# Other buffers for the fp8 rounding, a lower rank for the first scan, and earlier loads for the last FFN, in a kernel of four gated layers

## The chip, the cores and the metric

One core of one Trainium2 chip runs the kernel. The metric is the device time of one execution in microseconds; the figure of a kernel is the median over its runs. Of the kernel before there are three: 3698.0, 3705.31 and 3706.08 us, median 3705.31. A profile is one more execution, and it has a time of its own.

## The reference, cut to what matters

The input `x` has 4 batches of 512 rows by 512 columns; a context of 4 x 512 x 256 goes with it. Eight blocks follow one another, and each is added to `x` with a gate:

```python
x = x + tanh(g_xattn[0]) * mamba(ctx, layernorm(x), ...)      # layer 0: a selective scan
x = x + tanh(g_ffn[0])   * ffn_2to4(layernorm(x), ...)        # the two largest of each four kept
x = x + tanh(g_xattn[1]) * attention_from_ctx(layernorm(x))   # layer 1
x = x + tanh(g_ffn[1])   * ffn_ternary(layernorm(x), ...)
x = x + tanh(g_xattn[2]) * mamba(ctx, layernorm(x), ...)      # layer 2: a scan again
x = x + tanh(g_ffn[2])   * ffn_fp8(layernorm(x), ...)         # weights rounded to fp8 e4m3
x = x + tanh(g_xattn[3]) * attention_16_heads(layernorm(x), ctx, ...)   # layer 3
x = x + tanh(g_ffn[3])   * bitlinear_ffn(layernorm(x), ...)   # quantized rows, b1, gelu, layernorm, b2
```

The part of the two `mamba` blocks that is a recurrence (convolution, `u`, `dt`, and 16 states for each of 512 channels over 512 positions) depends on the context alone, not on `x`. So the kernel can compute it at any time before its layer. In the fp8 FFN each weight is rounded to three bits of mantissa (`w.astype(float8_e4m3fn)`). The last FFN works row by row: layer norm, quantization, a product, `b1` and gelu, a layer norm with `gamma` and `beta`, quantization, a second product, `b2`.

## The kernel before, in words

**The main flow** goes over eight stages, called heads: (layer group, batch) in the order (0,0), (0,1), (1,0), (0,2), (1,1), (0,3), (1,2), (1,3). A stage of group 0, `f01`, does the FFN of layer 0, the attention and the FFN of layer 1. A stage of group 1, `f23`, does the fp8 FFN of layer 2 and the attention of layer 3. In the profile the stages begin at about 200, 718, 1137, 1568, 1972, 2399, 2734 and 3158 us; a prologue with the scan of (0,0) stands ahead of them, and a tail from 3584 us, with the last FFN of batch 3, behind them. I call them stage 0 to stage 7.

**Three side lists** run along with the main flow, and `tick(w)`, which the main flow calls after each piece of its own work, feeds them: `side` (the scans of the seven other heads, `mamba_scan`, then the preparation of the last FFN's weights; in stages 6 and 7 the last FFN itself, `l3f`), `pres` (the preparations of the scans, `mamba_pre`) and `prep` (36 fp8 roundings, `to_fp8`, called by `l2f_prep`). Each list has a rate; `tick` adds `w` times the rate to the list's credit and takes steps of the list's generator until the credit is used up. A step costs what its `yield` says. `pres` runs at 0.25, but at 1.0 while the scan that heads `side` still lacks its preparation (`waits()`); `side` at 0.75 takes no step meanwhile but gathers credit; `prep` runs at 0.15. Before a head begins, `finish` traces whatever its scan or preparation still lacks, at once. `nxt.start` (L662 to L666) calls it inside the last product of the FFN of layer 1, then adds the scan's result to `x` (`xmamba`, L649); `nxt.turn` transposes the next input.

**The order in the engines' queues** is not the order of the code. Tile, the compiler layer, schedules all traced instructions with a model of their times: when an engine is free in the model it takes, of the instructions that are ready, the one with the lowest priority number, and that number counts up with each traced instruction. `tick` adds `BEHIND = 1000` to it for `prep`, and for `side` in all stages but the first; `copy` (L247) adds 200 in the first stage and 60 later. On the chip each queue then runs in the order so fixed, and each wait is a semaphore. All loads and most stores are issued by SP, a queue that does nothing else.

**Buffers.** A tile belongs to a tag of a pool, and a tag has a fixed number of buffers. Tag `wr` of pool `wr` (4 buffers of 128x512 f32) takes every raw weight that `unit` loads on its first use (L265), until it is split into a rounded part (ACT, L256) and a rest (POOL and DVE in turn, L257). `to_fp8` takes two of the same four: `raw` (L288) and `m` (L290); it works with DVE (L290), ACT (L293), DVE twice (L294, L295), and stores `raw` with `copy`. Tag `mt` of pool `m` (4 buffers of the same size) belongs to `mamba_pre`: the convolution (L484, L486), `u` (L491), stored to DRAM and loaded again for four matmuls into the bank `xd` (L508), and so on to `dt`, `du` and `y` (L564, L566). The state steps of a scan are L581 (ACT), L582 (POOL), L583 and L584 (DVE), L602 (POOL).

**The last FFN.** `l3f` works on 128 rows, a token tile, at a time. Of a tile's steps the first half goes up to gelu, the second half from there to the store; the first half of one tile is traced in turn with the second half of the tile before. `x` is loaded into `xl` (2 buffers, L1135) just ahead of its use at L359; `b1`, `gamma`, `beta` and `b2` are loaded by `rep` (5 buffers, L1115) just ahead of theirs (L1158, L1188, L1189, L1213). Its weights, 8 tiles, and its token tiles are in one pool, `l3f`. The tail calls the same function with a pool of its own, `tail`, which is opened when the pools of stage 7 are closed.

A pool that is placed on bytes of closed pools waits, as Tile is used here, for every user of those pools.

Of the kernel before, what the change touches and what calls it, by code (L numbers as in the profile page):

```python
# [10 lines left out]
F32 = mybir.dt.float32  # L11
# [12 lines left out]
NT = S // 128  # L24
# [30 lines left out]
BEHIND = 1000  # L55
# [17 lines left out]
def tile_flamingo(ctx: ExitStack, tc: tile.TileContext, I, out):  # L73
# [63 lines left out]
    phase = [0]  # L137

    def tick(w):

        waits = lambda: side and any(k == (*side[0][0], "pre") for k, _ in pres)
        for q, r, i in ((pres, 1.0 if waits() else RATE_PRE, 0), (prep, RATE_FP8, 2), (side, rate[0], 1)):
            credit[i] += w * r
            behind = BEHIND if q is prep or q is side and phase[0] else 0
            while q and credit[i] > 0 and not (q is side and waits()):
                tc.cur_priority += behind
                try:
                    credit[i] -= next(q[0][1])
                except StopIteration:
                    q.pop(0)  # L150
                tc.cur_priority -= behind
            if not q:
                credit[i] = 0.0
# [130 lines left out]
    def to_fp8(dst, src):  # L284


        raw = T(wrp, [128, 512], F32, "wr")
        sy.dma_start(raw, src)  # L288
        m = T(wrp, [128, 512], F32, "wr")
        v.tensor_scalar(  # L290
            m.bitcast(I32), raw.bitcast(I32), 0x7F800000, 0x00400000, op0=ALU.bitwise_and, op1=ALU.bitwise_or
        )
        s.activation(raw, raw, AF.Copy, scale=2.0**-20)  # L293
        v.scalar_tensor_tensor(raw, m, 1.5 * 2.0**-6, raw, op0=ALU.max, op1=ADD)  # L294
        v.scalar_tensor_tensor(raw, m, 1.5 * 2.0**-6, raw, op0=ALU.max, op1=SUB)  # L295
        copy(dst, raw)
# [175 lines left out]
    def mamba_pre(l, b, mp, pp=None):  # L472

        M = lambda tag, shape=(128, 512), dt=F32: T(mp, list(shape), dt, tag)
        po = l * PAR_MW
        ud = []
        for d in range(4):
            if pp:
                xi = xin[l, b, d]
            else:  # L480
                xi = M("mt")
                copy(xi, xin[l, b, d])
            cv = pp.tile([128, 512], F32, tag="cv", name=nm("cv"), bufs=2) if pp else mbps()
            s.activation(cv, xi, AF.Identity, scale=cw[l][:, d * 4 + 3 : d * 4 + 4], bias=cw[l][:, 16 + d : 17 + d])  # L484
            for j in (1, 2, 3):
                v.scalar_tensor_tensor(  # L486
                    cv[:, j:], xi[:, : 512 - j], cw[l][:, d * 4 + 3 - j : d * 4 + 4 - j], cv[:, j:], op0=MUL, op1=ADD
                )
            u = pp.tile([128, 512], F32, name=f"u{d}") if pp else M("mt")
            s.activation(u, cv, AF.Tanh)  # L490
            v.scalar_tensor_tensor(u, u, 1.0, cv, op0=ADD, op1=MUL)  # L491
            if pp:
                ud.append(u)
            else:
                ud.append(dram("u", [128, 512], F32))
                copy(ud[d], u)
            yield 2.6
        xw = M("mt")
        sy.dma_start(xw[:, :320], I[f"M{l}_xp"][0])
        xd = mbps("xd")  # L500
        for d in range(4):
            if pp:
                u = ud[d]
            else:
                u = M("mt")
                copy(u, ud[d])
            c = slice(d * 80, d * 80 + 80)
            pe.matmul(xd[:80], xw[:, c], u, start=d == 0, stop=d == 3)  # L508

        xf = M("mt")  # L510
        s.copy(xf[:80], xd[:80])
        st = M("mt", (128, 512), FR)
        s.copy(st[:80], xd[:80])
        v.tensor_tensor(st[64:80], xd[64:80], st[64:80], op=SUB)
        bcd = dram("bc", [32, 512], F32)
        keep(bcd[0:16], xf[16:32])
        keep(bcd[16:32], xf[48:64])
        dw = unit_dtw(l, mp)
        dtb = lambda d: par[:, po + PAR_M["db"] + d : po + PAR_M["db"] + d + 1]
        Dc = lambda d: par[:, po + PAR_M["D"] + d : po + PAR_M["D"] + d + 1]  # L520
        if pp:
            sc = []
            for d in range(4):
                ps = bank("y", "dtp")
                pe.matmul(ps, dw[:80, 0, d * 128 : d * 128 + 128], st[:80], start=True, stop=True)
                t = pp.tile([128, 512], F32, tag="t", name=nm("t"), bufs=2)
                s.activation(t, ps, AF.Abs, bias=dtb(d))
                s.activation(t, t, AF.Exp, scale=-1.0)
                dt = M("dt")
                s.activation(dt, ps, AF.Relu, bias=dtb(d))  # L530
                ac = pp.tile([128, 512], F32, tag="ac", name=nm("ac"), bufs=2)
                log1p(t, ac, mbps)
                v.scalar_tensor_tensor(dt, ac, LP_K, dt, op0=MUL, op1=ADD)
                du, y = M("du"), M("y")
                g.tensor_tensor(du, dt, ud[d], op=MUL)
                g.tensor_scalar(y, ud[d], Dc(d), 0.0, op0=MUL, op1=ADD)
                sc.append((dt, du, y))
            mst[l, b] = bcd, sc
            return
        ysc[l, b] = [dram("y", [128, 512], F32) for d in range(4)]  # L540
        sc = []
        tmp = dram("dtp", [128, 4, 512], F32)
        for d in range(4):
            ps = mbps("dtp")
            pe.matmul(ps, dw[:80, 0, d * 128 : d * 128 + 128], st[:80], start=True, stop=True)
            x = M("mt")
            s.activation(x, ps, AF.Identity, bias=dtb(d))
            keep(tmp[:, d], x)
        yield 1.0
        for d in range(4):  # L550
            dt = M("mt")
            copy(dt, tmp[:, d])
            t = M("mt")
            s.activation(t, dt, AF.Abs)
            s.activation(t, t, AF.Exp, scale=-1.0)
            s.activation(dt, dt, AF.Relu)
            ac = M("mt")
            log1p(t, ac, mbps)
            v.scalar_tensor_tensor(dt, ac, LP_K, dt, op0=MUL, op1=ADD)
            r = [dram("st", [128, 512], F32) for i in range(2)]  # L560
            copy(r[0], dt)
            u = M("mt")
            copy(u, ud[d])
            g.tensor_tensor(dt, dt, u, op=MUL)  # L564
            copy(r[1], dt)
            g.tensor_scalar(u, u, Dc(d), 0.0, op0=MUL, op1=ADD)  # L566
            copy(ysc[l, b][d], u)
            sc.append(r)
            yield 3.4
        mst[l, b] = bcd, sc  # L570
# [523 lines left out]

    def l3f(b, lp, ws, ps_of=mbps, tail=None):

        nbuf = {"rep": 5, "Y": 2, "q16": 2, "qT": 1, "yT": 4, "sq": 1, "xl": 2}
        if tail:
            nbuf = {"rep": 1, "Y": 4, "q16": 4, "qT": 2, "yT": 8, "sq": 1}

# [3 lines left out]
        def smallL(n):  # L1104
            return lp.tile([128, n], F32, tag="sm", name=nm("sml"), bufs=32 if tail else 16)

        kept = {}

        def rep(n, f):

            if (n, f) in kept:
                return kept[n, f]
            tag = f"rep{n}{f}" if tail else "rep"
            r = lp.tile([128, 512], F32, tag=tag, name=nm("rep"), bufs=nbuf["rep"])
            sy.dma_start(r, I["L3_" + n][512 * f : 512 * f + 512].partition_broadcast(128))  # L1115
            if tail:
                kept[n, f] = r
            return r

        def turned(x, tag):  # L1120

# [7 lines left out]
        def token(t):  # L1129

            if tail:
                x = tail[t]
            else:
                x = L("xl", [128, 512], F32)
                sy.dma_start(x, xsc[b * NT + t])  # L1135
            rs, _ = ln_stats([x], smallL)
            yield 0.7, 1.6
            y = L("Y", [128, 2048], F32)
            z = y[:, 0:512]
            s.activation(z, x, AF.Identity, scale=rs[:, 0:1], bias=rs[:, 1:2])  # L1140
# [11 lines left out]
            for f in range(4):  # L1152
                c = slice(f * 512, f * 512 + 512)
                b1r = rep("b1", f)
                ps = ps_of("l1")
                for k in range(4):
                    pe.matmul(ps, xq[:, k * 128 : k * 128 + 128], ws["w1", k][:, f], start=k == 0, stop=k == 3)  # L1157
                v.scalar_tensor_tensor(y[:, c], ps, sc[:, 1:2], b1r, op0=MUL, op1=ADD)  # L1158
                if f % 2:
                    h = slice((f - 1) * 512, f * 512 + 512)  # L1160
                    s.activation(y[:, h], y[:, h], AF.Gelu, accum_out=m2[:, f // 2 : f // 2 + 1])
                yield 0.7, 1.1
            yield HALF, 0.0

            v.tensor_tensor(m2[:, 2:3], m2[:, 0:1], m2[:, 1:2], op=ADD)
# [14 lines left out]
            for f in range(4):  # L1180
                c = slice(f * 512, f * 512 + 512)
                ga, be = rep("gamma", f), rep("beta", f)
                if tail and f % 2:
                    v.scalar_tensor_tensor(y[:, c], y[:, c], m2[:, 2:3], ga, op0=ADD, op1=MUL)  # L1184
                    v.scalar_tensor_tensor(y[:, c], y[:, c], m2[:, 3:4], be, op0=MUL, op1=ADD)  # L1185
# [32 lines left out]
        gens = [token(t) for t in range(NT)]  # L1218
        if not tail:

            old = iter(())
            for q in gens + [iter(())]:
                new = iter(lambda: next(q, (HALF, 0.0))[0], HALF)
# [76 lines left out]
    mctx.close()  # L1300
    with tc.tile_pool(name="l3f", bufs=2) as lp:
        ws3 = l3f_weights(lp)
        for b in range(2):
            side.append(((b,), l3f(b, lp, ws3)))
        rate[0] = RATES[6]
        f23(heads[6], heads[7])
        finish((1,))
        side.append(((2,), l3f(2, lp, ws3)))
        rate[0] = RATES[7]
        f23(heads[7], None)  # L1310
        finish((2,))
        with psum(t=6), tc.tile_pool(name="tail", bufs=2) as tp2:
            list(l3f(3, tp2, ws3, lambda n: bank("t", n), heads[7].xs))

# [86 lines left out]
```

## Time and profile before

| what | us |
|---|---|
| median of 3 runs | 3705.31 (3698.0 to 3706.08) |
| time of the profiled execution | 3685.68 |
| its span, first to last instruction | 3683.9 |
| busy in the span: PE, DVE, ACT, POOL | 3112.8, 2541.4, 1983.4, 1722.2 |
| mean granted clock of TensorE | 0.928 |

PE is TensorE's matmuls, PEld its weight loads, DVE VectorE, ACT ScalarE, POOL GpSimd, SP the queue that issues DMAs. A line of a group or of the timeline gives line, engine, operation, out<-in. In square brackets of the timeline stands how long the engine was idle before the instruction, and after the arrow what ended that. A line of the table by stage gives, for a stretch of the span, each engine's busy us and its number of instructions, then the granted clock, the share of the DMA engines' time and GB/s.

### The profile page before, as it was taken

How to read it: one execution, taken by the hardware profiler on the slowest of the kernel's cores; microseconds unless marked ns; L12 is line 12 of the kernel's file. 1: busy time of each engine (PE TensorE's matmuls, PEld its weight loads, DVE VectorE, ACT ScalarE, POOL GpSimd, SP SyncE). 2: the span in 40 equal slices, each digit the busy share in tenths (PEclk: the TensorE clock that was granted, in tenths of full speed). 3: DMA queues.
4: the chain of work that ended last, by engine and by line, in shares of the span. 5: the costliest groups of instructions: out<-in, count | busy, mean ns of one | idle time of the engine just before them, and what ended most of it. 6: DMA issues, size and time to landing. Idle time of an engine off the chain costs nothing. (4 is left out here: it accounts for less than half of the span.)

```text
span 3683.9 us, 40258 instructions
## 1 busy us (share of the span) xinstructions
PE 3112.8 (84%) x12216; PEld 1979.4 (54%) x12216; DVE 2541.4 (69%) x4162; ACT 1983.4 (54%) x4405; POOL 1722.2 (47%) x1351
## 2 busy tenths in 40 slices
PE   7785875889778788899888778899999998898985
PEld 3364444565556545475565545475767554564542
DVE  7957856789688787887678878855334455454437
ACT  6455355354545667544544656543435666366644
POOL 5515856637556785744665778700101122222112
PEclk9997887999899899999999899999999999999997
DMA  8577567876876564385676543287664343554310
GB/s 272 186 264 255 182 197 257 287 250 210 272 246 208 189 187 135 108 292 189 211 243 216 169 157 106 90 296 261 227 209 163 120 135 95 166 172 122 110 42 31
DMA packets 310232, 693.10 MB, mean 188 GB/s; under 512 B 31712, under 2 KB 33120, under 8 KB 310016
## 3 DMA queue, kind: packets, MB, share of 16 engines
q1 hardware_dynamic: 256176, 589.86, 47.3%
q10 hardware_dynamic: 53840, 100.68, 9.2%
q8 instruction: 97, 1.59, 0.2%
q14 instruction: 119, 0.97, 0.1%
HBM read 525.46 MB, written 164.95 MB: 187 GB/s over the span
## 5 line engine op out<-in xcount | busy, mean ns | idle before, releaser
L581 ACT ACTIVATE mb<-dt,nA 128x512 f32<-128x512 f32 x512 | 347.1, 689 | 398.2 <-DVE db12x L584 52.0
L333 POOL TENSOR_TENSOR sm<-sm,mhalf 128x8 f32<-128x8 f32 (+4 forms) x96 | 138.8, 1446 | 483.2 <-DVE sm L363 174.1
L678 PE MATMUL gate<-xT,w 128*128 128x512 f32 x624 | 266.9, 428 | 75.4 <-ACT w L256 40.1
L985 PE MATMUL po<-pt,v 128*128 128x512 f32 x512 | 277.9, 631 | 28.3 <-ACT pt L824 22.3
L807 PE MATMUL S<-k,q 128*128 128x512 f32 x512 | 264.9, 620 | 22.2 <-ACT P L814 19.8
L814 ACT ACTIVATE P<-S,st,sm 128x512 f32<-128x512 f32 x256 | 199.9, 783 | 119.1 <-DVE st L812 117.5
L679 PE MATMUL gate<-xT,w 128*128 128x512 f32 x624 | 258.7, 415 | 1.4 <-DVE xT L257 1.4
L402 PE MATMUL acc<-w,hf 128*128 128x512 f32 x512 | 233.0, 614 | 25.6 <-DVE hf L705 14.3
L678 PE MATMUL up<-xT,w 128*128 128x512 f32 x624 | 246.7, 395 | 4.1 <-ACT w L256 4.0
L679 PE MATMUL up<-xT,w 128*128 128x512 f32 x624 | 245.6, 394 | 0.0
L808 DVE TENSOR_REDUCE st<-S 128x1 f32<-128x512 f32 x256 | 173.2, 684 | 92.9 <-PE S L807 91.2
L1003 PE MATMUL down<-wo,h 128*128 128x512 f32 x512 | 231.9, 603 | 0.7 <-DVE x L430 0.7
L333 POOL TENSOR_TENSOR sml<-sml,mhalf 128x1 f32<-128x1 f32 x32 | 18.5, 578 | 440.9 <-DVE sml L1174 229.9
L822 PE MATMUL pT<-ident,P 128*128 128x128 f32 x1024 | 168.7, 285 | 52.0 <-ACT P L814 27.3
L822 PEld LDWEIGHTS pT<-ident,P 128*128 128x128 f32 x1024 | 127.6, 146 | 136.3 <-ACT P L814 45.8
L681 PE MATMUL gate<-xT,w 128*128 128x512 f32 x432 | 181.3, 420 | 14.0 <-POOL w L257 13.8
L678 PEld LDWEIGHTS gate<-xT,w 128*128 128x128 f32 x624 | 125.0, 200 | 116.0 <-ACT w L256 41.8
L402 PEld LDWEIGHTS acc<-w,hf 128*128 128x128 f32 x512 | 99.0, 196 | 155.6 <-issue 113.3
L681 PE MATMUL up<-xT,w 128*128 128x512 f32 x432 | 169.2, 392 | 3.2 <-DVE w L257 3.2
L824 ACT COPY pt<-pT 128x512 f32<-128x512 f32 x256 | 145.9, 589 | 47.7 <-PE pT L822 46.5
L402 PE MATMUL acc<-w,h 128*128 128x512 f32 x352 | 159.7, 606 | 6.3 <-ACT fv L907 4.9
L336 PE MATMUL Q<-w,xT 128*128 128x256 f32 x512 | 156.7, 306 | 3.3 <-ACT xT L256 3.2
(288 smaller groups left out, 8971.9 us busy)
## 6 DMA issues: line engine op xcount, KB each, us to landing
bc<-dbc ACTq DMA_DIRECT2D x105, 512.0 KB, 5.7
w<-dL_g SPq DMA_DIRECT2D x81, 512.0 KB, 5.3
w<-dL_u SPq DMA_DIRECT2D x81, 512.0 KB, 4.6
w<-in_L_d_dram SPq DMA_DIRECT2D x68, 512.0 KB, 5.5
w<-dL_gu SPq DMA_DIRECT2D x48, 512.0 KB, 4.6
w<-dL_q SPq DMA_DIRECT2D x48, 512.0 KB, 5.1
rep<-in_L_b_dram SPq DMA_DIRECT2D x65, 256.0 KB, 3.9
dv<-fv ACTq DMA_DIRECT2D x64, 256.0 KB, 4.0
```

The source lines that it names most:

```text
L333: g.tensor_tensor(a, a, mhalf[:, :n], op=ALU.pow)
L402: pe.matmul(ps, h[:, c], w, start=first, stop=last)
L581: s.activation(ps, dt, AF.Exp, scale=nA[l][:, d * 16 + n : d * 16 + n + 1])
L678: pe.matmul(ps, wh[:, c], xT[k][:, 0], start=k == 0, stop=False)
L679: pe.matmul(ps, wh[:, c], xT[k][:, 1], start=False, stop=wl is None and k == 3)
L681: pe.matmul(ps, wl[:, c], xT[k][:, 0], start=False, stop=k == 3)
L807: pe.matmul(ps, q[:, c], k, start=True, stop=True)
L808: v.tensor_reduce(st[:, t : t + 1], ps, AX.X, ALU.max, negate=True)
L814: s.activation(p, ps, AF.Exp, scale=r, bias=m, accum_out=st[:, 8 + t : 9 + t])
L822: pe.transpose(ps[:, t * 128 : t * 128 + 128], pt[t][:, kt * 128 : kt * 128 + 128], ident)
L985: pe.matmul(po, vs[kt][:, c], u, start=kt == 0, stop=kt == 3)
L1003: pe.matmul(ps, hs[j][:, c], ws[j // 2][:, j % 2], start=j == 0, stop=j == 3)
```

## The change

`tick`: a `side` that waits for its preparation gathers no credit, and the first stage's scan is traced 1000 behind as well.

```diff
         for q, r, i in ((pres, 1.0 if waits() else RATE_PRE, 0), (prep, RATE_FP8, 2), (side, rate[0], 1)):
+            if q is side and waits():
+                continue
             credit[i] += w * r
-            behind = BEHIND if q is prep or q is side and phase[0] else 0
+            behind = BEHIND if q is not pres else 0
```

`to_fp8`: both buffers come from `mt`.

```diff
-        raw = T(wrp, [128, 512], F32, "wr")
+        raw = T(mp, [128, 512], F32, "mt")
         sy.dma_start(raw, src)
-        m = T(wrp, [128, 512], F32, "wr")
+        m = T(mp, [128, 512], F32, "mt")
```

`mamba_pre`: three `u` are loaded a step (2.6) ahead of the matmuls, the fourth a step of 1.3 ahead of its own.

```diff
         xw = M("mt")
         sy.dma_start(xw[:, :320], I[f"M{l}_xp"][0])
+        if not pp:
+
+            for d in range(3):
+                u = M("mt")
+                copy(u, ud[d])
+                ud.append(u)
+            yield 2.6
         xd = mbps("xd")
         for d in range(4):
-            if pp:
-                u = ud[d]
-            else:
+            if not pp and d == 3:
                 u = M("mt")
                 copy(u, ud[d])
+                ud.append(u)
+                yield 1.3
             c = slice(d * 80, d * 80 + 80)
-            pe.matmul(xd[:80], xw[:, c], u, start=d == 0, stop=d == 3)
+            pe.matmul(xd[:80], xw[:, c], ud[d if pp else 4 + d], start=d == 0, stop=d == 3)
```

`l3f`, outside the tail: `xl` has 3 buffers for 2 and `rep` 7 for 5; each vector is loaded one use ahead, `x` of the next token tile ahead of the second half of this one. The token tiles get a pool of their own, `tokens`, on top of the weights' pool, and it is closed before the tail's pool is opened.

```diff
-        nbuf = {"rep": 5, "Y": 2, "q16": 2, "qT": 1, "yT": 4, "sq": 1, "xl": 2}
+        nbuf = {"rep": 7, "Y": 2, "q16": 2, "qT": 1, "yT": 4, "sq": 1, "xl": 3}
...
+        def fetch(*vs):
+
+            if not tail:
+                for n, f in vs:
+                    ahead[n, f] = rep(n, f)
+
+        def fetch_x(t):
+            xls[t] = L("xl", [128, 512], F32)
+            sy.dma_start(xls[t], xsc[b * NT + t])
...
-                x = L("xl", [128, 512], F32)
-                sy.dma_start(x, xsc[b * NT + t])
+                x = xls[t]
             rs, _ = ln_stats([x], smallL)
             yield 0.7, 1.6
+            fetch(("b1", 0))
...
                 b1r = rep("b1", f)
+                if f < 3:
+                    fetch(("b1", f + 1))
...
+            if not tail and t + 1 < NT:
+                fetch_x(t + 1)
+            fetch(("gamma", 0), ("beta", 0))
             yield HALF, 0.0
...
                 ga, be = rep("gamma", f), rep("beta", f)
+                fetch(*((("gamma", f + 1), ("beta", f + 1)) if f < 3 else (("b2", 0),)))
...
+            fetch_x(0)
+            yield 2.0
...
         ws3 = l3f_weights(lp)
-        for b in range(2):
-            side.append(((b,), l3f(b, lp, ws3)))
...
+        with tc.tile_pool(name="tokens", bufs=2) as lq:
+            for b in range(2):
+                side.append(((b,), l3f(b, lq, ws3)))
...
         with psum(t=6), tc.tile_pool(name="tail", bufs=2) as tp2:
             list(l3f(3, tp2, ws3, lambda n: bank("t", n), heads[7].xs))
```

`rep` first looks into `ahead` and takes a vector out of it that has been loaded there.

More of the change, by code (lines that the diff above doesn't have):

```diff
@@ L1105, in smallL @@
             return lp.tile([128, n], F32, tag="sm", name=nm("sml"), bufs=32 if tail else 16)
-        kept = {}
+        kept, ahead, xls = {}, {}, {}
         def rep(n, f):
@@ L1112, in rep @@
                 return kept[n, f]
+            if (n, f) in ahead:
+                return ahead.pop((n, f))
             tag = f"rep{n}{f}" if tail else "rep"
@@ L1302, in tile_flamingo @@
         ws3 = l3f_weights(lp)
-        for b in range(2):
-            side.append(((b,), l3f(b, lp, ws3)))
[L1305 to L1311, printed above, removed]
+        with tc.tile_pool(name="tokens", bufs=2) as lq:
+            for b in range(2):
+                side.append(((b,), l3f(b, lq, ws3)))
+            rate[0] = RATES[6]
+            f23(heads[6], heads[7])
+            finish((1,))
+            side.append(((2,), l3f(2, lq, ws3)))
+            rate[0] = RATES[7]
+            f23(heads[7], None)
+            finish((2,))
         with psum(t=6), tc.tile_pool(name="tail", bufs=2) as tp2:
```

## The prediction

> **What bounds the kernel now.** I read the times of each stage first, then who waited for whom, then the timeline where a wait was long, and last the chain of waits. These are rows of the table by stage: us, then busy us (and instructions) of PE, PEld, DVE, ACT and POOL, the granted clock, the DMA share, GB/s.
>
> ```profile
> 606.00:636.00 30.00, 0.91 (x3) 0.50 (x2) 20.76 (x25) 16.86 (x43) 22.68 (x16) 0.55 0.65 211
> ...
> 718.00:1137.00 419.00, 355.54 (x1276) 236.07 (x1276) 342.97 (x496) 216.38 (x488) 235.40 (x172) 0.93 0.74 247
> ...
> 2399.00:2734.00 335.00, 324.39 (x1252) 224.26 (x1252) 150.22 (x277) 135.76 (x355) 24.12 (x17) 0.99 0.71 243
> 2734.00:3158.00 424.00, 386.92 (x1772) 242.34 (x1772) 209.61 (x495) 251.40 (x563) 90.04 (x78) 0.97 0.45 142
> 3158.00:3584.00 426.00, 396.66 (x1789) 245.21 (x1790) 203.79 (x470) 242.43 (x551) 82.84 (x69) 0.96 0.38 118
> 3584.00:3684.00 100.00, 51.76 (x217) 21.20 (x214) 77.83 (x167) 42.61 (x81) 27.94 (x24) 0.78 0.15 48
> ```
>
> PE bounds the long stages: stage 5 (2399 on), with no scan beside it, is 97% busy. Stages 6 and 7 leave PE idle for 67 of 850 us, and the tail is bound by DVE. Scans lengthen stages 0 to 4. In one stretch, 606 to 636, PE does nothing at all. So a change counts by the PE gaps that it closes or opens; the chain of waits begins only at 3520 us and says nothing of the rest.
>
> **Part 1, fp8 rounding out of the buffers `wr`.** This is the gap of 606, in PE's timeline and then in SP's, DVE's and ACT's:
>
> ```profile
> 605.75 0.40 PE L338 MATMUL K<-fw,fc 128*128 128x512 f32 x1
> 635.24 0.80 PE L678 MATMUL gate<-xT,w 128*128 128x512 f32 x1 [29.09 <-ACT w L256]
> ...
> 604.34 0.43 SPq L288 DMA_DIRECT2D wr<-in_L_u_dram  x1
> ...
> 631.14 0.33 SPq L265 DMA_DIRECT2D wr<-in_L_g_dram  x1
> ...
> 629.48 1.63 DVE L295 SCALAR_TENSOR_TENSOR wr<-wr,wr 128x512 f32<-128x512 f32 x1
> ...
> 634.57 0.62 ACT L256 CAST w<-wr 128x512 fp32r<-128x512 f32 x1 [1.34 <-DMA wr<-in_L_g_dram]
> ```
>
> The gate waits for the split of its weight, the split for the load of 631.14, and that load for the end (631.11) of a rounding whose raw block was asked for at 604.34. Two roundings held all four `wr`. With the roundings in `mt` the gap of 29.1 us goes. What is late next is the scan of (0,1): its last addition on POOL ends at about 630, the last of its products on POOL (L641) starts at 638.2, its result reaches `x` (L649) at 659.5, and the next gates start at 718.4. PE has 66.9 us of work from 606 to 718, so at most 112 - 66.9 = 45 us are to be had.
>
> Against this stands part 2. The scan comes later: its preparation's steps cost 2.6 + 1.3 = 3.9 units more, stage 0 spends some 440 us on 102 units up to `nxt.start` (4.3 us each), hence +17 us; nothing hides that, for `pres` runs at full rate and `side` waits for it. From then the scan needs what it needed: the additions of the seven scans take 207 to 316 us each, at rank 0 (first, 291 us) as at rank +1000 (second, 316 us). I therefore cost the rank at nothing: POOL covers it, which at that rank (stages 1 to 4) is 56 to 73% busy. So the gates of stage 0 end about 627 instead of 657, the product's rows fill PE until 665 (88 matmuls L402, 0.43 us apart: 38 us), `x` gets the scan's result at about 657 (630 + 17, and 10 us for store, load and L641), and the next gates follow 25 to 35 us later, at 682 to 692 (where no scan runs it took 44 us, 2690 to 2734, with PE's rows in between; the 10 to 20 less are my estimate). That is 26 to 36 us less. The roundings now take two of the four `mt` in turn with the preparation; its steps pay some of that back. I take **-25 us**, bounds -45 (PE never idle) and +41 (worked out under the rivals).
>
> The same move in stages 1 and 2 gains nothing, since no raw weight is loaded there, and slows roundings and preparations that share four buffers. The last rounding's L295 runs at 1088, the first gate that needs any at 1137: 49 us of cover. I take **0**, bounds 0 and +25: most roundings run from 826 to 1088, and if sharing stretches these 262 us by 74, the gates wait 74 - 49.
>
> The credit that `side` no longer gathers is 0.75 x 28.9 = 22 of 76.8, about 18 of the 64 state steps; `finish` traces them at `nxt.start`, without the 1000. It is cost at nothing too: POOL's pace sets the scan, not the place in the code. Without that cover they cost 18 x 2.75 us (eight additions in 22 us, the fastest stretch, 338 to 360) = 50 us, behind which PE has 38 us of rows.
>
> **Part 3, `u` ahead.** Before L508 PE and its weight loads sat idle 20.3 us for `mt<-du`, nine times in seven preparations; of the matmuls' own wait 8.6 us is that. A step of 2.6 units is some 10 us, a load lands in about 3 to 4. I take **-5 us**, bounds -15 and +5 (the bank `xd`, one of two for `mb`, is held 1.3 units longer; 11.0 us of waits for it by `db02x` stand in the same row).
>
> **Part 4, the last FFN's loads.** Waits in stages 6 and 7 (us in total, times, longest):
>
> ```profile
> ACT P L814 <- DVE st L812: 70.1, 29, 10.1
> ...
> DVE sml L359 <- DMA xl<-xsc: 47.0, 8, 10.1
> ...
> POOL Y L1188 <- DMA rep<-in_L_gamma_dram: 34.1, 15, 5.6
> ```
>
> One of the eight, in SP's, DVE's and PE's timeline:
>
> ```profile
> 2907.65 0.42 SPq L1215 DMA_DIRECT2D out_dram<-xl  x1
> ...
> 2911.64 0.33 SPq L1135 DMA_DIRECT2D xl<-xsc  x1
> ...
> 2915.54 0.69 DVE L359 BATCH_NORM_STATS2 sml<-xl 128x6 f32<-128x512 f32 x1 [7.91 <-DMA xl<-xsc]
> ...
> 2917.31 1.11 PE L822 MATMUL pT<-ident,P 128*128 128x128 f32 x4 [6.74 <-ACT P L814]
> ```
>
> With two `xl` the load follows the store of the tile before; DVE stands still in its queue, the maximum for the softmax (L808, L812) stands behind it, then ACT's exponential, then PE. A third buffer, loaded half a tile ahead, removes store and load from that. Of PE's gaps over 0.8 us these follow such a wait: 6.74 + 0.85 (2911), 1.27 (3035), 7.61 (3150), 8.89 + 0.85 (3376): 26.2. Behind waits for `b1`: 1.33 + 4.22 (3104, 3113) and 4.09 (3336): 9.6. Together 35.9.
>
> After such a gap the clock is low. In the table by stage the windows 2911:2923, 3150:3162 and 3377:3391 have clocks 0.57, 0.72 and 0.63, and 4.85 + 4.58 + 5.07 = 14.5 us of PE work that would take about half: 7 us more. The Trainium skill, "TensorE: Matmul & The Clock Gate", Part 1, says that for modelling the ramp costs under 1% of a typical span; by that the 7 would be left out and this part's value would be 24. The rows speak against it: the mean clock is 0.928 over the span.
>
> Of 43 us I take two thirds, **-28 us**: DVE's next wait is for PE's scores, and some of PE's gaps would be there a little later. Bounds -43 and 0. SP issues as many transfers as before; with seven `rep` it blocks less.
>
> **Part 5, the tail's pool.** It now lies on `tokens`, so it waits for that pool's last user too. SP's timeline:
>
> ```profile
> 3583.86 1.75 SPq L1115 DMA_DIRECT2D rep<-in_L_b_dram  x4
> ...
> 3588.81 0.34 SPq L1215 DMA_DIRECT2D out_dram<-xl  x1
> ```
>
> Today the tail's loads start as the last product of stage 7 ends (3583.80), its first L359 at 3584.49. The last token tile's store is issued at 3588.81 and lands at 3592.1. Waiting for it costs 3592.1 - 3584.5 = 7.6 us; nothing hides it, as everything in the tail follows. Bounds 0 (the tile done sooner) and +8. I take **+7**.
>
> **Sum:** -25 + 0 - 5 - 28 + 7 = -51 us. The profiled execution took 3685.7 (span 3683.9 and 1.8 around it), so 3635 there. The median lies 19.6 above that execution; I keep this difference: 3705.3 - 51 = **3654 us**.
>
> **Rivals.**
> - *The scan comes too late (slower).* In stage 0 a rounding holds a buffer from its load to the landing of its store, 241.5 to 270.6 = 29 us. If the preparation of (0,1), 247 to 327, has to wait out two of these, its scan starts at 338 + 17 + 58 = 413 and ends, after the same 291 us, at 704, not 629: L649 at about 734, the next gates at 759, 41 us after 718. With the roundings late in stage 2, +25, the sum is 41 + 25 - 5 - 28 + 7 = +40: **3745**. For it: four buffers for two users, on the one scan without slack (the second ends 961 for a need at about 1080). Against: the preparation has the lower priority number. It decides from a first addition of this scan (L602) later than about 388 (338 + 17 + 33); beyond 415 or so the kernel is slower.
> - *The loads were hidden anyway.* PE is 92% busy in stages 6 and 7; if the softmax chain only moves, part 4 gives 3 us: 3705 - 26 = **3679**.
> - *All of it comes.* -45 - 10 - 43 + 0 = -98: **3607**.
> - *It cancels.* The queues' order was fixed by modelled times, so that a gap of 29 us can return with another cause (the raw load also stands behind the scan's stores in SP); then -28 + 7 + 20: **3705**.
>
> **Chances.** Forecast 0.48 (its own range 3630 to 3685), loads hidden 0.17, scan late 0.20, all 0.08, cancels 0.07. About 0.2% (7 us) is what a measurement of this kernel can tell from no change. Faster by more: 0.48 + 0.17 + 0.08 = 0.73; within: 0.07; slower: 0.20. The range 3605 to 3725 leaves out half of "all" (0.04) and the larger part of "late" (0.14).
>
> **What would show it.** No PE gap near 606 ended by ACT L256 behind L295; next gates near 690. First addition of the first scan at 355 to 388. No wait of L359 for `xl`; stages 6 and 7 shorter by 28 together. Tail's first L359 behind the last `out_dram<-xl`. Wrong: a gap before `xmamba`'s transposes in stage 0, gates of stage 2 waiting for roundings, or PE gaps on L822 as long as now without a wait for `xl`.

## The result and the profile after

The kernel became slower. Its median over 20 runs is **3710.65 us** (3700.3 to 3719.94), that of the kernel before, over 20 runs beside them, 3701.06 (3691.7 to 3708.5). The ratio is 1.0025, with a 95% interval of 1.0017 to 1.0034.

The profiled execution took 3714.27 us (span 3712.5, mean granted clock 0.92). It lies 3.6 us above its median; that of before, 3685.68, lay 15.4 below the median of its 20 runs. So the two profiles differ by 28.6 us where the medians differ by 9.6, and a single profile says little on a stage's last few microseconds. How little, a second profile of the unchanged kernel shows (first experiment).

Each stage from its first gate matmul to that of the next (stage 7 to its last product):

| us | prologue | 0 | 1 | 2 | 3 | 4 | 5 | 6 | 7 | tail |
|---|---|---|---|---|---|---|---|---|---|---|
| before | 201.2 | 517.2 | 419.1 | 431.3 | 403.8 | 426.6 | 335.1 | 423.8 | 425.8 | 100.1 |
| after | 207.6 | 493.8 | 419.8 | 486.3 | 407.4 | 426.4 | 353.9 | 404.4 | 404.5 | 108.3 |
| difference | +6.4 | -23.4 | +0.7 | **+55.0** | +3.6 | -0.2 | +18.8 | -19.4 | -21.3 | +8.2 |
| forecast | 0 | -25 | 0 | 0 | 0 | 0 | 0 | -28 in | both | +7 |

The table by stage of after, in the columns known from before (a stretch in stage 0, then stage 2, stages 5, 6, 7 and the tail):

```profile
612.00:672.00 60.00, 0.00 (x0) 0.00 (x0) 43.59 (x51) 19.08 (x29) 52.86 (x44) 0.54 0.61 176
...
1121.00:1607.50 486.50, 380.61 (x1513) 235.41 (x1513) 375.00 (x586) 282.39 (x615) 296.04 (x233) 0.89 0.52 161
2441.00:2795.00 354.00, 333.06 (x1252) 227.76 (x1252) 192.33 (x321) 151.63 (x382) 84.14 (x62) 0.97 0.73 247
2795.00:3199.60 404.60, 383.74 (x1755) 241.39 (x1755) 206.84 (x486) 246.26 (x559) 90.61 (x78) 0.98 0.45 140
3199.60:3604.20 404.60, 389.86 (x1786) 242.28 (x1786) 206.01 (x477) 238.45 (x546) 82.44 (x69) 0.97 0.42 127
3604.20:3712.00 107.80, 53.70 (x240) 22.63 (x237) 79.02 (x169) 44.86 (x85) 27.91 (x24) 0.78 0.13 44
```

(The forecast's -5 for `u` was spread over stages 0 to 4.) Stages 6 and 7 gave PE's idle time back: 20.9 + 14.7 = 36 us are left of 37.1 + 29.3 = 66. Stage 5 is no longer free of scans: POOL is busy 84 us in it (62 instructions), before 24 (17). And in stage 0 PE still does nothing for 60 us, now in one piece, until the scan has ended. PE's timeline there, then POOL's:

```profile
605.50 6.17 PE L404 MATMUL acc<-w,h 128*128 128x512 f32 x14
672.65 0.90 PE L656 MATMUL xm<-ident,z 128*128 128x128 f32 x3 [60.98 <-POOL z L650]
```

```profile
660.72 1.26 POOL L611 TENSOR_TENSOR y<-y,db01x 128x512 f32<-128x512 f32 x1
662.06 1.27 POOL L591 TENSOR_TENSOR db10x<-du,bc 128x512 f32<-128x512 f32 x1
663.29 2.49 POOL L611 TENSOR_TENSOR y<-y,db01x 128x512 f32<-128x512 f32 x2
665.74 1.27 POOL L591 TENSOR_TENSOR db10x<-du,bc 128x512 f32<-128x512 f32 x1
671.34 2.49 POOL L650 TENSOR_TENSOR z<-z,y 128x512 f32<-128x512 f32 x2 [4.33 <-DMA y<-dy]
```

The gap of 29.1 us that waited for a weight's split is gone. PE runs through its gates and products and then stands before the transposes of `xmamba`: the scan's last addition (L611) ends at 665.8, store, load and product (L650) follow, and the next gates start at 701.5, 36 us after the scan's end.

**The loss is in stage 2**, where the fp8 FFN begins. PE's timeline (all lines with an idle time in brackets between 1146 and 1213), and the row of the page on these gates:

```profile
1162.39 4.74 PE L517 MATMUL xd<-mt,mt 128*80 128x512 f32 x6 [12.76 <-DVE db02x L593]
1169.73 2.00 PE L517 MATMUL xd<-mt,mt 128*80 128x512 f32 x2 [2.60 <-DMA mt<-du]
1179.26 0.80 PE L687 MATMUL gate<-xT,w 128*128 128x512 f32 x1 [7.53 <-DMA w<-dL_gu]
1192.24 0.79 PE L687 MATMUL gate<-xT,w 128*128 128x512 f32 x1 [7.12 <-DMA w<-dL_gu]
1199.02 0.47 PE L687 MATMUL gate<-xT,w 128*128 128x512 f32 x1 [0.61 <-DMA w<-dL_gu]
1212.76 0.76 PE L687 MATMUL gate<-xT,w 128*128 128x512 f32 x1 [9.86 <-DMA w<-dL_gu]
```

```profile
L687 PE MATMUL gate<-xT,w 128*128 128x512 f32 x624 | 269.5, 432 | 69.9 <-DMA w<-dL_gu 28.5
```

The gates wait for rounded weights that have only just been stored. Before, the first 100 us of this stage had no gate wait of over 1.2 us behind the first gate's, and the last rounding was done 49 us ahead of it. These are lines of before: the last step of the last rounding, the longest of those gate waits, and the row of stage 2.

```profile
1088.32 0.68 DVE L295 SCALAR_TENSOR_TENSOR wr<-wr,wr 128x512 f32<-128x512 f32 x1
...
1159.61 0.50 PE L678 MATMUL gate<-xT,w 128*128 128x512 f32 x1 [1.17 <-DVE t L748]
```

```profile
1137.50:1568.80 431.30, 364.70 (x1500) 230.51 (x1500) 359.82 (x549) 268.96 (x597) 306.37 (x242) 0.92 0.50 161
```

Now 17 of the 36 roundings run inside the stage, from 1171 to 1227. SP's timeline shows what they stood behind, and SP's own waits from 1125 to 1180 name it (us in total, times, longest):

```profile
1121.37 0.75 SPq L501 DMA_DIRECT2D mt<-in_M_xp_dram  x1
1122.22 0.83 SPq L249 DMA_DIRECT2D mt<-du  x1
...
1128.57 0.32 SPq L249 DMA_DIRECT2D mt<-du  x1
1164.42 0.33 SPq L290 DMA_DIRECT2D mt<-in_L_u_dram  x1
...
1175.70 0.32 SPq L316 DMA_DIRECT2D w<-dL_gu  x1
```

```profile
SPq L290 <- PE xd L517: 39.6, 2, 35.5
```

From 1121 the next preparation holds all four `mt`: its matrix (L501) and three `u` loaded ahead. They are released by the matmuls L517, which wait for the bank that the running scan holds, until 1162.4. For 35.5 us SP issues nothing, because the next transfer in its queue is the raw block of a rounding (L290) and wants one of these four buffers. Only then are the roundings done one after another, and each gate waits for its own.

Of the 55 us, 39 are idle time of PE (486.5 - 380.6 = 105.9, before 66.6) and 16 are more busy time (380.6 for 364.7 us). Only a part of the 16 goes with the lower clock (0.89 for 0.92). The stage has 1513 matmul records for 1500, because the matmuls of a second preparation now fall into it; by their own times these are 7.7 us. The matmuls that both profiles have in the stage take some 9 us longer.

The waits of stages 6 and 7, those that answer to the three shown of before:

```profile
ACT P L823 <- DVE st L821: 51.5, 32, 3.8
...
POOL Y L1216 <- DMA rep<-in_L_beta_dram: 6.1, 6, 2.1
POOL Y L1215 <- DMA rep<-in_L_gamma_dram: 3.4, 4, 1.1
```

There is no wait for `xl` at all, and the longest wait of the softmax's exponential fell from 10.1 to 3.8 us. The tail's first `rep` loads, by SP, and its first statistics, by DVE:

```profile
3611.63 0.34 SPq L1242 DMA_DIRECT2D out_dram<-xl  x1
3613.91 1.76 SPq L1126 DMA_DIRECT2D rep<-in_L_b_dram  x4
```

```profile
3614.06 0.69 DVE L361 BATCH_NORM_STATS2 sml<-x 128x6 f32<-128x512 f32 x1 [2.46 <-DMA out_dram<-xl]
```

Both wait for the landing of the last token tile's store: 9.7 and 9.9 us after stage 7's end (3604.2), where before it was 0.1 and 0.7.

### The profile page after: what moved, and what is told of

It is laid out like the page before. It is cut to its first block, busy times and chain, and to the rows that moved or that the text cites. A ratio compares the mean times of both kernels' runs of the same rounds, so it can differ in the third digit from the quotient of the medians.

```text
span 3712.5 us, 40289 instructions
## 1 busy us (share of the span) xinstructions
PE 3111.1 (84%) x12216; PEld 1983.8 (53%) x12216; DVE 2542.8 (68%) x4162; ACT 1983.2 (53%) x4399; POOL 1720.2 (46%) x1351
## 4 chain that ended last, share of the span: by engine, by line
PE 28%; DVE 8%; POOL 6%; DMA 4%; issue 3%; ACT 3%; SPq 0%; ACTq 0%; POOLq 0%; DVEq 0%
PE acc L404 3%; PE po L994 3%; PE S L816 3%; PE down L1012 3%; POOL y L611 2%; DVE mb L592 2%; PE pT L831 2%; PE l L1237 1%; PE gate L687 1%; PE gate L688 1%; PE up L688 1%; PE up L687 1%; PE Q L338 1%; PE l L1180 1%; PE Q L339 1%
## 5 line engine op out<-in xcount | busy, mean ns | idle before, releaser
L404 PE MATMUL acc<-w,hf 128*128 128x512 f32 x512 | 231.4, 611 | 16.7 <-DVE hf L714 13.3
L1012 PEld LDWEIGHTS down<-wo,h 128*128 128x128 f32 x512 | 96.1, 192 | 112.2 <-issue 104.6
```

What stands on the lines that cost most here:

```text
L404: pe.matmul(ps, h[:, c], w, start=first, stop=last)
L1012: pe.matmul(ps, hs[j][:, c], ws[j // 2][:, j % 2], start=j == 0, stop=j == 3)
```

## The experiments

All medians stand against runs of the kernel before on the same chip; the 95% interval of the ratio follows in brackets. Line numbers shift with the parts that a kernel has.

**How much two profiles of one kernel differ.** The kernel before, unchanged.

> The kernel before, unchanged, profiled once more: how far the stages of one and the same kernel differ between two executions. Stages 0 to 7 within 3 us each if the difference of 19 us between the profiled pair (28.6) and the medians (9.6) is chance spread over the program; one stage 10 us or more off if it sits in one place.

3697.75 us. The ten parts differ from the first profile by +3.8, -1.2, +2.4, -2.8, +2.0, +6.3, -0.8, -0.8, +2.9, +0.2. The gap of stage 0 is there again (29.79 us). So +55, +19, -41 and -23 are effects, and +6 in the prologue need not be one.

**Each part alone.** The diffs are those of "The change", one part each: the last FFN with its pools, the buffers of `to_fp8`, `tick`, and `mamba_pre`. The expectations speak of theories on the loss; the second one spells them out.

> Only the last FFN's part: third xl, seven rep, loads one use ahead, and the token tiles' own pool. Both theories agree here: stages 6 and 7 some 40 us shorter together (19.4 + 21.3 in the two traces), the tail 8 us longer, stages 0 to 5 as before. 3701 - 33 = 3668 us. If the order of the earlier stages moves by itself with any edit (a rival to all of this: the compiler's order is sensitive), stages 0 to 5 change by more than 10 us in sum.

> Only the roundings' buffers, taken from mt. Theory A (the roundings, in the preparations' four buffers, come too late for stage 2): some 15 of 36 roundings run after stage 2 has begun, its gates wait for their weights, stage 2 about 45 us longer, stage 0 about 25 us shorter without the 29 us gap: 3715 to 3725 us. Theory B (the scan's rank and the credit not gathered make everything late, the roundings only follow): no more than 5 roundings in stage 2, stage 2 within 10 us of before, 3670 to 3685 us. Theory C (u ahead fills mt with xw and three u and keeps a bank): as B here.

> Only the credit and the rank of the first scan. Theory A: little, within 10 us of 3701; the first addition of the first scan at about 340 as before. Theory B: first addition near 380, all scans later, stage 2 about 40 us and stage 5 about 19 us longer: 3740 us or more, less what stage 0 gives.

> Only the u loaded ahead in the preparations. Theory A and B: -5 to +10 us; the first scan starts some 17 us later for the 3.9 units more (355). Theory C: first scan 40 us later, matmuls L508's successor wait 10 us and more for the scan's bank in stage 2, 3720 us or more.

| part alone | us | ratio | stage 0 | 2 | 5 | 6 + 7 | tail |
|---|---|---|---|---|---|---|---|
| before | 3699.2 | | 517.2 | 431.3 | 335.1 | 849.6 | 100.1 |
| last FFN | 3664.38 | 0.9912 [0.9892, 0.9931] | 514.5 | 430.4 | 337.1 | **804.3** | 109.0 |
| roundings | 3736.36 | 1.0108 [1.0091, 1.0126] | 491.8 | **482.2** | 335.4 | 852.8 | 100.0 |
| `tick` | 3673.05 | 0.9934 [0.9919, 0.9949] | **483.4** | 424.3 | 331.2 | 851.8 | 100.1 |
| `u` | 3709.34 | 1.0028 [1.0017, 1.0039] | 513.7 | 429.7 | 336.6 | 851.2 | 100.4 |

The last FFN's loads are worth 35 us, 45 in stages 6 and 7 less 9 in the tail. Stage 3, not in the table, is 20 us longer with `tick` alone, 17 with `u` alone and 4 in the whole change; the runs do not explain this. The roundings carry the loss of stage 2 by themselves, without `u` loaded ahead: 17 of them run there, up to 1231, and a gate waits 28 us:

```profile
1190.57 0.76 PE L678 MATMUL gate<-xT,w 128*128 128x512 f32 x1 [28.28 <-DVE mt L290]
```

So the block of 35.5 us behind three `u` is not what the loss needs: here SP waits at most 7.2 us at a time before a rounding's load (from 1120 to 1215), and stage 2 is 51 us longer all the same.

`tick`, costed at nothing, closes the 29 us gap of stage 0 without any new buffer; PE then stands before the scan, as in the whole change:

```profile
660.60 0.90 PE L649 MATMUL xm<-ident,z 128*128 128x128 f32 x3 [34.76 <-POOL z L643]
```

The four sum to -35 + 37 - 26 + 10 = -14 us; the whole change costs +10. So some 23 us come from parts that work against each other.

**Is stage 2 lost because of `mt` there, or because of the roundings' way at all?** The roundings take `mt` only while stage 0 is traced, and `wr` afterwards:

```diff
+        p, tag = (wrp, "wr") if phase[0] else (mp, "mt")
-        raw = T(wrp, [128, 512], F32, "wr")
+        raw = T(p, [128, 512], F32, tag)
```

and `m` in the same way.

> The roundings alone, in mt while stage 0 is traced and in wr from stage 1 on. If the loss of the run with the roundings alone (+37 us) comes from the shared mt in stages 1 and 2, stage 2 returns to about 431 us, no rounding runs after the gates begin to need it, stage 0 keeps its 25 us, and the time is about 3675 us. If the loss comes from what the roundings do in stage 0 (scan 20 us later, and all after it), stage 2 stays near 480 us: 3735 us.

3663.23 us, 0.9902 [0.9878, 0.9926]: the roundings' +37 turned into -37. Stage 0 takes 482.3, stage 2 427.9, and the last rounding runs at 1090, as before the change. It is the shared buffers of stages 1 and 2.

**Does it help to trace the roundings early?** All in `mt`, with twice the rate, so that all are traced before stage 2:

```diff
-RATE_FP8 = 0.15
+RATE_FP8 = 0.32
```

> The roundings alone in mt, but at a rate of 0.32 for 0.15, so that all 36 are traced before stage 2 instead of 17 to 19. If the trace order of the mt buffers is what holds them back (a rounding that is traced behind the preparation of (1,1) gets its buffers behind it), none is left for stage 2 and stage 2 is about 435 us; stages 0 and 1 pay some for it, in sum about 3690 us. If four mt buffers are too few in number for roundings and preparations, stage 2 stays over 465 us or stages 0 and 1 grow by as much: 3735 us.

3701.31 us, 1.0004 [0.9991, 1.0016]. Stage 2 comes back to 445.2 (one rounding in it, done at 1163), so it was the late tracing that put them behind the preparation's tiles. But stage 0 takes 510.4, for 491.8 at the old rate: the first scan now starts at 383 and ends at 689 us, and PE stands 56.67 us before `xmamba`. Half of what stage 2 wins back is lost there, and the four buffers serve both no better than `wr` did.

**The parts that gained, together; and the whole change without one part.** First `tick` and the last FFN; then all but the roundings (`tick`, `u`, last FFN); then all but `u`.

> The two parts that were faster alone, the tick and the last FFN, without the roundings' move and without u ahead. If they add up: 3699 - 26 - 35 = 3638 us. If the tick's gain is an accident of the order (its 34 us in stage 0 lost when anything else changes), 3665 us.

> The whole change but the roundings' move. If the roundings are what turned it into a loss: tick, last FFN and u as each alone, 3700 - 26 - 35 + 10 = 3649 us, stage 2 near 430 us, no rounding after its first gates. If u ahead is as much to blame (four mt held by xw and three u): first addition of the first scan beyond 360 and 3670 us or more.

> The whole change but u ahead. If the first addition of the first scan is late by what each part costs alone (tick 4, roundings 21, u 19 us: 384 in the changed kernel), it now comes at about 363, the stretch without matmuls before x gets the scan's result shrinks from 61 to about 40 us, stage 0 is about 475 us; stage 2 stays near 480 us for the roundings: 3685 to 3695 us. If u ahead is harmless beside the others: 3705 to 3715 us.

3639.56 us, 0.9839 [0.9813, 0.9866]: the best version found, 61 us under the kernel before, which is the sum of its parts (26 + 35). With `u` 3644.32, 0.9849 [0.9833, 0.9865]. With `tick`, roundings and last FFN, 3722.96, 1.0059 [1.0039, 1.0078], although the sum of these three alone is -24 and 3685 to 3695 were expected. Stage 2 takes 523.1 us in it, with three gate waits of 28.60, 36.24 and 11.47 us; why it is 41 us more than with the roundings alone is not settled:

```profile
1185.41 0.79 PE L680 MATMUL gate<-xT,w 128*128 128x512 f32 x1 [28.60 <-DMA w<-dL_gu]
1228.00 0.76 PE L680 MATMUL gate<-xT,w 128*128 128x512 f32 x1 [36.24 <-DMA w<-dL_gu]
```

So `u` ahead costs 5 to 10 us where the roundings are not in its buffers (the 5 lie within the intervals) and saves some 12 where they are.

Stage 5 goes with how far the last scan reaches into it. In twelve of the 17 profiles the scan's last addition ends before stage 5 begins, or 1 us into it, and the stage takes 327 to 337 us. In three it ends 52 to 54 us into it, and the stage takes 344 to 346 (the two last kernels above with the roundings as their only part, and the rank alone below). In two it ends 75 us into it, and the stage takes 353.9 and 355.0: the whole change, and the whole change without the roundings, the two that have both `tick` and `u`. No edit was made for this alone, so it is a regularity, not a test.

**Do the two gains of stage 0 add?** `tick`, the roundings in `mt` in stage 0 only, the last FFN.

> Tick, last FFN, and the roundings in mt while stage 0 is traced, in wr later. Alone the tick gave 26 us and this placing of the roundings 36 us, nearly all of both in stage 0. If stage 0 is bound by its first scan once the 29 us gap is gone, they don't add up: stage 0 at 470 to 485 us as with each alone, 3630 to 3650 us. If they add up: 3600 us.

3652.38 us, 0.9865 [0.9845, 0.9884]: not 37 us better than `tick` and the last FFN, but 13 worse. Stage 0 takes 498.6 (482.4 without the roundings), and PE's longest wait behind the prologue in any profile stands in it:

```profile
680.12 1.12 PE L650 MATMUL xm<-ident,z 128*128 128x128 f32 x4 [80.27 <-POOL z L644]
```

What ends stage 0 is seen by putting the kernels side by side (us; first scan's first and last addition, by their starts, then the next gates):

| kernel | first | last | gates | gates - last |
|---|---|---|---|---|
| before | 338 | 629 | 718.4 | 89 |
| `tick` | 342 | 653 | 684.0 | 31 |
| roundings in stage 0 | 360 | 660 | 689.4 | 30 |
| `tick`, last FFN | 345 | 654 | 686.4 | 33 |
| `tick`, roundings, last FFN | 370 | 665 | 697.7 | 33 |
| `tick`, roundings in stage 0, last FFN | 368 | 676 | 705.4 | 30 |
| after | 384 | 665 | 701.5 | 37 |

Once the gap of 29 us is closed, by whichever part, the gates follow the scan's last addition by 30 to 37 us (28 to 43 in the other kernels that have one of these parts), and what counts is when the scan ends. That is its start plus 281 to 311 us in this table, so most of a later start is paid. A second remedy for the gap gains nothing and delays the scan.

**What sets the scan's length?** `tick` and the last FFN, with the first stage's rate doubled:

```diff
-RATES = [0.75, 0.75, 0.75, 0.75, 0.75, 0.75, 0.75, 0.75]
+RATES = [1.5, 0.75, 0.75, 0.75, 0.75, 0.75, 0.75, 0.75]
```

> Tick and last FFN (3639.6 us) with the rate of side in stage 0 at 1.5 for 0.75. If the place of the scan's steps in the trace sets its pace: the scan of (0,1), 345 to 654 now, ends near 620, the gap of some 35 us before x gets its result closes, stage 0 is about 460 us: 3615 us. If POOL's pace sets it, as the prediction said: ends near 650, no difference within 8 us.

3729.86 us, 1.0077 [1.0052, 1.0102]. The first scan still takes 345 to 651, 306 us for 309: tracing its steps earlier moves nothing. What does set its length this does not show; POOL is busy 68% of these 306 us and DVE 70%. The kernel is 90 us slower than with the single rate, which neither expectation had. The time is lost afterwards: the second scan runs from 698 to 945 beside the main flow of stage 1 (462.9 us, 427.5 with the single rate), 13 roundings slip into stage 2 (478.2 for 427.7), and stage 3 takes 447.6 for 418.8. The roundings are in `wr` here, so shared buffers are not the only thing that can make them late; what does it in this kernel is not settled.

**Rank or credit?** The two edits of `tick`, one at a time: `behind = BEHIND if q is not pres else 0`, and `if q is side and waits(): continue`.

> Only the rank of the first scan (+1000), credit as before. If the rank closes the 29 us gap, by letting the splits of the weights and the gates' work go ahead of the scan: about 3675 us, no gap over 10 us ended by ACT L256 near 606. If the credit does it: 3700 us.

> Only the credit that a waiting scan no longer gathers, rank as before. If the rank is what counts: 3700 us, the gap near 606 still there, the last 18 state steps of the first scan in one go at the end of stage 0. If the credit counts: 3675 us.

The rank alone: 3691.41, 0.9982 [0.9967, 0.9998], for 3675 expected if the rank counts. The gap is gone and stage 0 takes 489.4, but stage 2 takes 444.7 and stage 5 343.7. The credit alone: 3723.18, 1.0057 [1.0037, 1.0077], for 3700; the gap is still there, and stages 1 and 2 take 438 and 440:

```profile
628.02 0.80 PE L680 MATMUL gate<-xT,w 128*128 128x512 f32 x1 [33.49 <-ACT w L258]
```

So it is the rank that closes the gap. -6 and +26 make -26 together: why stages 1, 2 or 5 lose under one edit alone and not under both is not settled.

**Is the tail's loss the wait of its pool?** `tick` and the last FFN, with the tail's pool waiting for single tiles of the pools under it instead of all their users:

```diff
-        with psum(t=6), tc.tile_pool(name="tail", bufs=2) as tp2:
+        with psum(t=6), tc.tile_pool(name="tail", bufs=2, reuse_waits="tile") as tp2:
```

> Tick and last FFN (3639.6 us), and the tail's pool waits tile by tile for earlier users of its own bytes, not for every user of the pools beneath. If the tail's 8 us more come from the wait for the last token tile's store, the tail falls from 108 to about 100 us: 3632 us. If they come from something else in the tail (its vectors' loads, the order of its four tiles), no difference: 3640 us.

3639.86 us, 0.9838 [0.9821, 0.9856], the same as without it. The tail takes 105.8 for 108.3. In its profile SP issues the tail's loads straight behind the last token tile's store, without waiting for it to land:

```profile
3539.50 0.34 SPq L1235 DMA_DIRECT2D out_dram<-xl  x1
3539.94 1.83 SPq L1119 DMA_DIRECT2D rep<-in_L_b_dram  x4
```

But that is 7.9 us after stage 7's end (3532.0). The pool's wait is 2.5 of the 8 us. The rest goes with the place of the last token tile's last steps in the queues, ahead of the tail's first. In DVE's queue the tail's first statistics stand behind them, although nothing else holds them back now:

```profile
3537.93 0.75 DVE L1233 SCALAR_TENSOR_TENSOR Y<-l,sml,rep 128x512 f32<-128x512 f32 x1 [4.44 <-PE l L1230]
3538.72 0.75 DVE L1234 SCALAR_TENSOR_TENSOR xl<-Y,tg,xl 128x512 f32<-128x512 f32 x1
3539.39 0.69 DVE L361 BATCH_NORM_STATS2 sml<-x 128x6 f32<-128x512 f32 x1
```

Before, L359 ran at 3584.49, ahead of that tile's L1213 (3586.47). The table by stage shows the same work move: 240 matmul records stand in the tail after, 217 before, and 20 of these are transposes and products of the last token tile. The order was not changed by an edit, so this part is argued from the traces.

## Why the prediction was wrong

Its sign was wrong. By its own steps:

- **"The same move in stages 1 and 2 gains nothing ... 49 us of cover. I take 0, bounds 0 and +25": this step failed.** It cost 55 us. The 49 us were read from a kernel in which the roundings ran ahead of their turn, and they could do so because in stage 1 nobody else used `wr` until 1077. (That no raw weight is loaded in stages 1 and 2 was a wrong reading: 16 blocks of `L_q` pass through `wr` from 1077 to 1319, but only as the last roundings end.) The move takes away just that. The buffers went in the order of tracing: 17 roundings are traced late, by `finish`, after the next preparation's tiles, and did not run ahead of them. The bound of +25 stretched the roundings' duration; what changed was their start. With the roundings left in `wr` after stage 0 the loss is gone, with an earlier tracing nearly so.
- **-25 for the gap of stage 0: measured -23**, but as a balance, so that the close number is luck. The scan started 46 us later (by the start delays of the parts alone: `tick` 4, roundings 21, `u` 19) and not 17: `u` at 17 was right, the buffers' sharing was given no number in the forecast. The scan's additions took 281 us, not 291, and the gates came 37 us after the last, not 40; 6 us of the 46 were a longer prologue.
- **The rank "at nothing": wrong as a statement on the change, right on the scan.** That the place in the code does not set the scan's length holds (306 us for 309 with the rate doubled); that POOL's pace does was not shown (POOL is busy 66 to 72% of the first scan in every profile). But the rank moves everything that the scan stood ahead of, and closed the same 29 us gap that part 1 was to close. I never asked what the main flow would do with the places that the scan gave up.
- **`u`, -5, bounds -15 and +5: alone +10**, outside the bounds. The waits for `mt<-du` fell as meant: of the matmuls' own from 8.6 us to 4.4 with `u` alone and 5.5 in the whole change, the weight loads' from 11.7 to 7.4 there. The bank took them back in the whole change (waits of the same matmuls for `db02x` and `db10x`: 5.1 us before, 16.7 after). What `u` alone loses 10 us to, the runs did not settle; its profile is longer in stages 1 (+10) and 3 (+17). With `tick`, it costs 20 us in stage 5, and these go with a last scan that ends 75 us into that stage. Beside the roundings it saves 12.
- **The last FFN, -28 of 43: measured -41 in stages 6 and 7** (-45 alone). 31 us are idle time of PE, 10 are shorter busy time. Of the 10, by the trace's record of the granted clock, 5 are less time lost to the lower clock (PE's work at a clock of 0.5, counted half: 20.9 us before, 15.8 after); the other 5 go with 20 matmuls of the last token tile that now run in the tail. The mechanism was right; taking two thirds for "DVE's next wait" was too careful. As with the 7 us of clock that I counted there, gaps cost twice: in stage 2 the same count rises from 23.9 to 32.6 us, by 2% of the stage. The Trainium skill, "TensorE: Matmul & The Clock Gate", Part 1, puts the ramp under 1% of a typical kernel span for modelling. Over the span of before PE works 352 us at a clock of 0.5; counted half, as an estimate, that is 176 us or 5%, so this case speaks against leaving it out here.
- **The tail, +7: measured +8.** The size was right, by luck: the pool's wait, which was to be the cause, is 2.5 us of it, and the rest goes with the last token tile's own steps.
- **The rivals.** "The scan comes too late" had its sign and half its place: the first addition came at 384, just under the 388 from which it was to decide, and PE stood 61 us before `xmamba`, and stage 0 was 23 us shorter all the same. Its other half, roundings late in stage 2, was priced at +25 and cost 55, without the first half. I had tied the two together; they are independent. "The loads were hidden anyway" is answered by the last FFN alone, which gains 35 us. "It cancels" named 3705, near what came, but by a gap in stage 0 that returns and takes the gain there away; stage 0 kept its 23 us, so that nearness is luck.

With +55 in place of 0, the sum of -51 would have been +4 and the median 3709: this step alone turns the sign. The 19 us of stage 5 are then nearly paid by the 13 that the last FFN gave beyond its forecast.

## What to carry to other kernels

Slack that a profile shows belongs to the buffers in use there: before a tile is moved to another tag, list that tag's users in the order of tracing and ask which of them the moved work can no longer overtake, and what stands behind the blocked load in its queue. When two edits close the same gap, cost the second at nothing or less, and look at once for what ends the stage when the gap is gone (here the end of the scan, some 300 us after its start). Try the parts alone: of four, two were worth 61 us together, and the other two turned that into a loss.

## What the runs showed of the hardware

The same operation on DVE takes longer beside POOL. The rounding's last step, 128x512, in after, once from 1174 to 1230 and once from 200 to 1120 (ns: shortest, median, longest):

```profile
L297 DVE SCALAR_TENSOR_TENSOR mt<-mt,mt x16: 681/691/694, 1176.9 to 1227.1; 128x512 f32<-128x512 f32 x16
```

```profile
L297 DVE SCALAR_TENSOR_TENSOR mt<-mt,mt x18: 659/1086/1683, 262.1 to 1110.9; 128x512 f32<-128x512 f32 x18
```

From 1176 to 1228 POOL did nothing; earlier, with scans running, the median is 1.09 us for 0.69. Taken one by one over the whole trace, the 20 of these steps that no POOL instruction overlaps took 659 to 694 ns, and the six during which POOL worked throughout took 1071 to 1683. This agrees with the Trainium skill, "SBUF — State Buffer", "Who interferes with whom": a VectorE instruction with two inputs in SBUF, as this one has, contends with a GpSimd instruction that reads SBUF. So roundings that were moved into a stretch without POOL ran faster each and still came too late.
